# A convolution stage with one more shift copied by ScalarE, shifts loaded in two parts, and evictions in fixed places

## The chip, the core and the metric

The kernel runs on one core of a Trainium2 chip. A core has five engines that run side by side, each strictly in its own order: TensorE (PE in the profile, with its weight loads as PEld), VectorE (DVE), ScalarE (ACT), GpSimd (POOL) and SyncE (SP, which here only issues transfers). They wait for each other by semaphores. Sixteen DMA engines carry the transfers that SP and POOL issue. The metric is device time in microseconds for one execution; the time of a kernel is the median of its runs.

## What is computed

The input x has shape (4, 512, 512, 16): four images, 16 channels. Two layers are added to it.

```python
# layer 0: long convolution by FFT, all 16 channels mixed at each frequency
X = jnp.fft.rfft2(_gn(x), s=(1024, 1024), axes=(-3, -2))
Y = jnp.einsum('...hwi,ijhw->...hwj', X, H_full)      # H_full from a rational filter
x = x + jnp.fft.irfft2(Y, s=(1024, 1024), axes=(-3, -2))[..., :512, :512, :]
# layer 1: 3x3 convolution divided by the input's and kernel's norms, then arccos and tanh
x = x + _L1_conv_ref(_gn(x), kernel, bias, radius)
```

`_gn` is a group normalisation over eight groups of two channels. All arithmetic is in fp32.

## The kernel before

The kernel has four stages in time: the filter (up to some 3.6 ms), the forward transform of x along one axis, the convolution stage `conv_phase`, and the last stage with the second layer. The change lies in `conv_phase` alone.

`conv_phase` works through 513 rows (one row frequency each; the first is done as two). For a row, the other axis is split into two steps of a transform, 128 frequencies `f` by 8 taps, so that the long convolution becomes, at each `f`, a small product of input (`xe`) with filter (`gh`) over channels and taps. The parts of a row's work:

- `load_x`, `load_g`: the row of x and of the filter come from DRAM, through SP's queue.
- `turn_x` (ACT, then DVE): the row's own turning factors.
- `x_part`: four transforms of x on PE (tile `px`, two per buffer); each pair is evicted into `xe[:, 0]`, after b = 1 and after b = 3.
- `x_late` (POOL): `xe[:, 0]` is stored to DRAM (`xf_d`, first half); four multiplications into `xu`, one into `xl` and an addition make a turned copy `xl`, which is stored as the second half.
- Shifts: `xe` has eight slots t. Slot t needs slot 0 shifted by 16t partitions, with the partitions that fall off the end taken from `xl`. Slot 4 (64 partitions) is copied by ACT in two halves (`half_shift`, line 809: half 0 reads `xe`, half 1 reads `xl`). The other six are read back from `xf_d` by two loads of three slots each (`load_xe`, line 815), which need both stores.
- `g_part`: 32 matmuls on PE into `pg`, in four groups k, each evicted by two copies (c = 0 and 1) into `gh`.
- `mix`: 128 matmuls on PE, four groups of 32 (here M0 to M3) into `pm` (two buffers); each group is evicted into `yf`.
- `over_q`: 16 transposes in four groups into `pz`; for each group ACT copies one half to `zq` and DVE does five additions or subtractions (lines 874 to 878) into `z`. After the fourth group POOL computes `zd` and `z` (lines 882, 884).
- `over_g`: eight matmuls into `py`, one eviction to `yo`, and a store by POOL.

The evictions of `xe`, `gh`, `yf` and `yo`, 15 a row, go through `evict`, which gives every third to DVE and the others to ACT (lines 724 to 729):

```python
flip[0] += 1
if flip[0] % 3 == 0:
    nc.vector.tensor_copy(dst, src)
else:
    nc.scalar.copy(dst, src)
```

`step(n)` writes the parts of several rows in four quarters k: mixes of row n, `g_part` of row n + 1, `over_q` of row n - 1, `x_part` and `x_late` of row n + 2, `half_shift` of row n + 2 at k = 2 and 3, `over_g` of row n - 2. This program order is not the final one: when the program is built, the framework's scheduler puts each engine's instructions into an order of its own, and from then on that order is fixed. In the built program before, PE runs one mix group, then a `g_part` group, then a group of transposes, then px or py, and so on; ACT's copy of `xl` (half 1) stands ahead of evictions of `yf`, `gh` and `yo`. Buffers that matter: three of `xe`, two of `gh`, two of `pm`, three of `pg`, and three shared by `px`, `pz` and `py`.

Of the kernel before, what the change touches and what calls it, by code (L numbers as in the profile page):

```python
# [46 lines left out]
P = 128  # L47
N = 512
B = 4
C = 16  # L50
# [7 lines left out]
XF = F * 2 * B  # L58
XP = XF + 128
# [131 lines left out]
def load_const(nc, pool, cst, name, shape=None):  # L191
    src = cst[name]
    t = pool.tile(list(src.shape), F32, name=f"c_{name}")
    nc.sync.dma_start(out=t, in_=src)
    return t


def dram(t, row, offset, *dims):

    pitch = t.shape[1]  # L200
    lead = [[pitch, t.shape[0]]] if row is None else []
    return bass.AP(tensor=t.tensor, offset=t.offset + (row or 0) * pitch + offset,
                   ap=lead + [list(d) for d in dims])
# [492 lines left out]
def conv_phase(tc, cst, g_d, x_d, y_d):  # L696
    nc = tc.nc
    with ExitStack() as ctx:
# [15 lines left out]
        late = load_const(nc, cp, cst, "late").rearrange("p (v f) -> p v f", v=3)  # L714

        xf_d = [tc.dram_tile([16 * C, XP], F32, name=f"xf_d{n}") for n in range(4)]
# [2 lines left out]
        rows = [(0, 0, 0), (0, 0, 1)] + [(n // P, n % P, None) for n in range(1, N)]  # L719
        n_rows = len(rows)  # L720
        state = {}
        flip = [0]

        def evict(dst, src):
            flip[0] += 1
            if flip[0] % 3 == 0:
                nc.vector.tensor_copy(dst, src)  # L727
            else:
                nc.scalar.copy(dst, src)  # L729
# [13 lines left out]
        def load_x(n):  # L743
            rc, r, plane = rows[n]
            x = io.tile([P, B, 8 * C], F32, name="x")
            t, w = x.rearrange("p b x -> p (b x)"), B * 8 * C
            if plane is None:
                nc.sync.dma_start(out=t, in_=dram(x_d[rc], r, 0, [w, P], [1, w]))
            else:
                nc.gpsimd.memset(t[S:], 0.0)  # L750
                nc.sync.dma_start(out=t[:S], in_=dram(x_d[rc], r, plane * S * w, [w, S], [1, w]))
            state["x", n] = x
# [16 lines left out]
        def x_part(n, b):  # L769

            if b == 0:

                state["xe", n] = xep.tile([P, 8, F, 2, 2, 2], F32, name="xe")
            if b % 2 == 0:
                state["px"] = ps_f.tile([P, 2, F, 2], F32, name="px", tag="full")
            px = state["px"]
            nc.tensor.matmul(px[:, b % 2].rearrange("p f c -> p (f c)"), state["x", n][:, b],  # L777
                             state["dfs", n], start=True, stop=True)
            if b % 2:
                evict(state["xe", n][:, 0, :, b // 2], px.rearrange("p k f c -> p f c k"))  # L780
            if b == B - 1:
                del state["x", n], state["dfs", n]

# [22 lines left out]
        def half_shift(n, half):  # L806

            dst, src = ((slice(0, 64), state["xe", n][64:, 0]), (slice(64, P), state["xl"][:64]))[half]
            nc.scalar.copy(state["xe", n][dst, 4].rearrange("p f h c k -> p (f h c k)"),  # L809
                           src.rearrange("p f h c k -> p (f h c k)"))  # L810

        def load_xe(n):
            src = xf_d[n % 4]
            for t in (1, 5):
                nc.sync.dma_start(
                    out=state["xe", n][:, t : t + 3].rearrange("p t f h c k -> p t (f h c k)"),
                    in_=bass.AP(tensor=src.tensor, offset=src.offset + t * C * XP,
                                ap=[[XP, P], [C * XP, 3], [1, XF]]),
                )

        def g_part(n, j):


            if j % 4 == 0:
                state["pg"] = [ps_g.tile([P, 4, F], F32, name=f"pg{c}", tag="pg") for c in range(2)]
            g, pg = state["g", n], state["pg"]
            for c in range(2):
                half = slice(64 * c, 64 * c + 64)
                nc.tensor.matmul(pg[c][:, j % 4], g[half, j], dg[half], start=True, stop=True)  # L829
            if j == 3:  # L830
                state["gh", n] = ghp.tile([P, F, 2, C], F32, name="gh")
            if j % 4 == 3:
                for c in range(2):
                    evict(state["gh", n][:, :, c, j - 3 : j + 1], pg[c].rearrange("p j f -> p f j"))
            if j == C - 1:
                del state["g", n]

        def mix(n, g):

            if g % 8 == 0:  # L840
                state["pm"] = ps_m.tile([P, 8, 8, 2 * B], F32, name="pm")
            xe, gh, pm = state["xe", n], state["gh", n], state["pm"]
            for q in range(4):
                f = g + 32 * q
                nc.tensor.matmul(  # L845
                    pm[32 * q : 32 * q + 32, g % 8], gh[:, f].rearrange("p c j -> p (c j)"),
                    xe[:, :, f].rearrange("p t h c k -> p t (h c k)"), start=True, stop=True,
                )
            if g == 7:

                state["y", n] = yp.tile([P, 16, 32, 4], F32, name="yf")
            if g % 8 == 7:
                evict(state["y", n][:, :, g - 7 : g + 1].rearrange("p t g x -> p g t x"),
                      pm.rearrange("p g t (h x) -> p g (t h) x", h=2))
            if g == 31:
                del state["xe", n], state["gh", n]

# [30 lines left out]
        def over_g(n, k):  # L888

            rc, r, plane = rows[n]  # L890
            if k == 0:
                state["py"] = ps_f.tile([P, 2, 2, 8, C], F32, name="py", tag="full")
            z, d, py = state["z", n], state["zd", n], state["py"]
            odd, c2 = k // 2, k % 2
            for half in range(2):
                s0 = 2 * half + odd
                if s0 % 2 == 0:
                    zs = z[:, :, s0 + c2]
                elif s0 == 1:
                    zs = (d[:, :, 0], z[:, :, 5])[c2]  # L900
                else:
                    zs = (z[:, :, 4], d[:, :, 1])[c2]
                nc.tensor.matmul(  # L903
                    py[64 * half : 64 * half + 64, odd], ig[:, s0, c2],
                    zs.rearrange("p (t h) j -> p h t j", h=2),
                    start=(c2 == 0), stop=(c2 == 1),
                )
            if k < 3:
                return
            del state["z", n], state["zd", n]  # L910
            yo = yop.tile([P, 4 * P], F32, name="yo")
            evict(yo.rearrange("p (x j t) -> p x j t", x=4, j=C), py.rearrange("p o h t j -> p (o h) j t"))
            if plane is None:
                nc.gpsimd.dma_start(out=dram(y_d[rc], r, 0, [4 * P, P], [1, 4 * P]), in_=yo)
            else:
                for half in range(2):
                    nc.gpsimd.dma_start(
                        out=dram(y_d[rc], r, (64 * half + 32 * plane) * 4 * P, [4 * P, 32], [1, 4 * P]),
                        in_=yo[64 * half : 64 * half + 32],
                    )  # L920

        def step(n):


            def row(k):
                return 0 <= n + k < n_rows

            if row(3):
                load_x(n + 3)
            if row(2):  # L930
                load_g(n + 2)
            if row(1):
                load_xe(n + 1)
            for k in range(4):
                if row(0):
                    for g in range(8):
                        mix(n, 8 * k + g)
                if row(1):
                    for j in range(4):
                        g_part(n + 1, 4 * k + j)  # L940
                if row(-1):
                    for t in range(4):
                        over_q(n - 1, 4 * k + t)
                if row(2) and k == 0:
                    for m in range(2, B):
                        x_part(n + 2, m)
                    x_late(n + 2)
                if row(2) and k >= 2:
                    half_shift(n + 2, k - 2)
                if row(3) and k == 1:  # L950
                    turn_x(n + 3)
                if row(3) and k == 3:
                    for m in range(2):
                        x_part(n + 3, m)
                if row(-2) and k in (1, 2):
                    for m in range(2):
                        over_g(n - 2, 2 * (k - 1) + m)

        for n in range(-3, n_rows + 2):
            step(n)  # L960
# [479 lines left out]
```

## Time and profile before

| What | Value |
|---|---|
| median of three runs | 16334.61 us (16324.06 to 16345.95) |
| profiled execution | 16344.5 us, span 16342.7 us |
| busy, share of the span | PE 91%, DVE 64%, POOL 62%, ACT 54% |
| convolution stage | about 4630 to 13530 us |
| reads from DRAM, writes | 3030.71 MB, 1477.31 MB |
| loads of xe from xf_d | 1026 issues of 1536 KB |
| stores to xf_d | 1026 issues of 448 KB |
| one ACT eviction of 128x512 (gh) | 585 ns |
| one DVE eviction of 128x512 (gh) | 688 ns |
| one ACT copy of 64x1024 (slot 4) | 1.05 us |

The span is the time that the profile covers; the execution's own time lies 1.8 us above it. Busy shares are means over stages with different work, so the convolution stage has to be read by itself. In the lines of the time line the columns are start, duration, engine, source line, operation, tile written and read, shapes, and in brackets how long the engine stood idle before it and what released it. A released wait says who came last. "issue" stands for idle time in which nothing that the profile shows was waited for.

### The profile page before, as it was taken

To read this page: it belongs to the slowest core of one execution; us is meant where nothing else is said; L and a number is where in the kernel's file an instruction comes from. 1 tells how busy PE (TensorE), PEld (TensorE's weight loads), DVE (VectorE), ACT (ScalarE), POOL (GpSimd) and SP (SyncE) were. 2 spreads that over 40 slices of the span, in tenths; PEclk is the share of its full clock that TensorE was granted. 3 is DMA by queue.
4 is the path that set the end of the run, shared out by engine and by line. 5 is a ranking of instruction groups with operands and counts; after the bars stand their busy time and mean duration, and the time that the engine had idled before them with its cause. 6 is when DMAs were issued, how large, how long until landed. Compare 5 with 4: busy or idle time off the path is not lost. (4 is left out here: it accounts for less than half of the span.)

```text
span 16342.7 us, 538107 instructions
## 1 busy us (share of the span) xinstructions
PE 14869.0 (91%) x232588; PEld 10969.0 (67%) x232588; DVE 10396.8 (64%) x20763; ACT 8766.8 (54%) x17007; POOL 10169.4 (62%) x9645
## 2 busy tenths in 40 slices
PE   7999999999988888888888888888888888988888
PEld 5555555554566667766666676667666667877777
DVE  8999999984545555555555555555555552457887
ACT  4666666653345555555555555555555551027888
POOL 7777777763456666666666666666666660247766
PEclk8999999999999999999999999999999999989999
DMA  4888888888878888888888888888888886884531
GB/s 138 239 244 249 241 242 245 245 241 261 250 276 329 323 329 329 329 330 329 329 331 324 330 328 327 328 325 327 330 331 328 326 325 236 319 297 164 168 109 67
DMA packets 2914643, 4542.93 MB, mean 278 GB/s; under 512 B 126114, under 2 KB 2094460, under 8 KB 2801422
## 3 DMA queue, kind: packets, MB, share of 16 engines
q1 hardware_dynamic: 2703070, 3836.37, 67.9%
q0 software_dynamic: 172336, 605.00, 9.3%
q10 hardware_dynamic: 36864, 67.13, 1.2%
q8 instruction: 1831, 30.00, 0.7%
q14 instruction: 542, 4.44, 0.1%
HBM read 3030.71 MB, written 1477.31 MB: 276 GB/s over the span
## 5 line engine op out<-in xcount | busy, mean ns | idle before, releaser
L845 PEld LDWEIGHTS pm<-xe,gh 128*32 128x32 f32 x131328 | 2001.2, 111 | 1446.2 <-issue 1163.4
L845 PE MATMUL pm<-xe,gh 128*32 128x64 f32 x131328 | 2373.7, 222 | 650.1 <-issue 314.8
L829 PE MATMUL pg<-c_dg,g 64*128 64x128 f32 x32832 | 2599.4, 289 | 308.3 <-ACT gh L729 192.5
L874 DVE TENSOR_TENSOR z<-zq,pz 128x256 f32<-128x256 f32 x2052 | 861.6, 420 | 2952.0 <-ACT zq L873 2950.0
L829 PEld LDWEIGHTS pg<-c_dg,g 64*128 64x128 f32 x32832 | 2134.2, 190 | 573.3 <-ACT gh L729 245.9
L729 ACT COPY gh<-pg 128x512 f32<-128x512 f32 x2567 | 1446.9, 585 | 1296.4 <-PE pg L829 1293.9
L459 PE MATMUL pt<-ev_in,c_todd 128*128 128x512 f32 x4096 | 1924.7, 609 | 9.5 <-DMA ev_in<-g_d 9.5
L389 DVE RECIPROCAL dn<-dn 128x256 f32<-128x256 f32 x1024 | 1722.9, 1724 | 17.6
L390 POOL TENSOR_TENSOR sp<-m,dn 128x512 f32<-128x512 f32 x1024 | 1301.2, 1271 | 592.6 <-DVE dn L389 556.1
L809 ACT COPY xe<-xl 64x1024 f32<-64x1024 f32 x513 | 539.0, 1051 | 1883.2 <-POOL xl L800 1883.2
L727 DVE COPY gh<-pg 128x512 f32<-128x512 f32 x1537 | 1056.7, 688 | 663.5 <-PE pg L829 660.3
L866 PE MATMUL pz<-c_ident,yf 128*128 128x128 f32 x8208 | 1376.5, 291 | 19.4 <-issue 13.0
L798 POOL TENSOR_TENSOR xu<-xe,c_late 128x256 f32<-128x256 f32 x2052 | 1373.8, 692 | 20.5 <-DVE xe L727 6.4
L459 PEld LDWEIGHTS pt<-ev_in,c_todd 128*128 128x128 f32 x4096 | 728.9, 190 | 910.3 <-issue 773.0
L418 ACT COPY st<-pg 128x256 f32<-128x256 f32 x2048 | 616.8, 391 | 1301.6 <-PE pg L407 1301.6
L407 PEld LDWEIGHTS pg<-c_dinv,sp 64*128 64x128 f32 x16384 | 1005.6, 196 | 442.2 <-ACT sp L395 232.6
L800 POOL TENSOR_TENSOR xl<-xl,xu 128x1024 f32<-128x1024 f32 x513 | 1208.9, 2357 | 40.2
L407 PE MATMUL pg<-c_dinv,sp 64*128 64x128 f32 x16384 | 1108.3, 287 | 60.3 <-ACT sp L395 44.6
L882 POOL TENSOR_TENSOR zd<-z 128x512 f32<-128x512 f32 x513 | 654.1, 1275 | 781.6 <-DVE z L874 781.6
L903 PE MATMUL py<-z,c_ig 128*64 128x256 f32 x6156 | 1127.4, 397 | 6.6 <-issue 2.2
L1283 PE MATMUL pc<-l_band,xn 128*128 128x160 f32 (+2 forms) x6144 | 1075.8, 333 | 52.0 <-DVE e_o L1338 51.9
L777 PE MATMUL px<-dfs_n,x 128*128 128x256 f32 x4104 | 1080.4, 387 | 12.7 <-DMA c_late<-k_late 11.5
(211 smaller groups left out, 29585.0 us busy)
## 6 DMA issues: line engine op xcount, KB each, us to landing
xe<-xf_d SPq DMA_DIRECT2D x1026, 1536.0 KB
g<-g_d SPq DMA_DIRECT2D x511, 1024.0 KB
g_d<-st SPq DMA_DIRECT2D x256, 1024.0 KB
ev_in<-g_d SPq DMA_DIRECT2D x1024, 256.0 KB
g_d<-ot SPq DMA_DIRECT2D x1024, 256.0 KB
xf_d<-xe POOLq DMA_DIRECT2D x513, 448.0 KB, 8.3
xf_d<-xl POOLq DMA_DIRECT2D x513, 448.0 KB, 6.4
x_d<-xo SPq DMA_DIRECT2D x128, 1024.0 KB
```

Of the source, the lines that this page charges most:

```text
L389: nc.vector.reciprocal(dn, dn)
L390: nc.gpsimd.tensor_mul(w["sp"][:, v], w["m"][:, v], bc(dn, 2, [P, 2, 2, P]))
L407: nc.tensor.matmul(pg[u][:, n, k].rearrange("p a x -> p (a x)"), w["sp"][q, n, k, c, :], dinv[q, 2 * kp + k, c, :], start=(c == 0), stop=( ...
L459: nc.tensor.matmul(pt, todd[:, c, kc, hh * P : hh * P + P], ev[:, kc, c], start=(kc == 0), stop=(kc == 1),)
L729: nc.scalar.copy(dst, src)
L777: nc.tensor.matmul(px[:, b % 2].rearrange("p f c -> p (f c)"), state["x", n][:, b], state["dfs", n], start=True, stop=True)
L798: nc.gpsimd.tensor_mul(u[:, :, h, c], xe[:, :, h, 1 - c], bc(late[:, 1 + c], 2, [P, F, 2]))
L800: nc.gpsimd.tensor_add(xl.rearrange("p f h c k -> p (f h c k)"), xl.rearrange("p f h c k -> p (f h c k)"), u.rearrange("p f h c k -> p (f ...
L829: nc.tensor.matmul(pg[c][:, j % 4], g[half, j], dg[half], start=True, stop=True)
L845: nc.tensor.matmul(pm[32 * q : 32 * q + 32, g % 8], gh[:, f].rearrange("p c j -> p (c j)"), xe[:, :, f].rearrange("p t h c k -> p t (h c k ...
L866: nc.tensor.transpose(pz[:, t % 4].rearrange("p v q x -> p (v q x)"), y[:, at].rearrange("p g x -> p (g x)"), ident)
L903: nc.tensor.matmul(py[64 * half : 64 * half + 64, odd], ig[:, s0, c2], zs.rearrange("p (t h) j -> p h t j", h=2), start=(c2 == 0), stop=(c ...
```

## The change

- `evict` no longer counts; each call says whether DVE does it. On DVE: the eviction of px after b = 3, `gh` for c = 1, `yf` of M0 and M1, and `yo`: eight a row. On ACT: px after b = 1, `gh` for c = 0, `yf` of M2 and M3: seven a row. Before it was five and ten.
- Slot 2 (a shift by 32 partitions) is no longer loaded but copied by ACT in four pieces of 32 partitions (`quarter_shift`). Pieces 0 to 2 read `xe`, piece 3 reads `xl`. They are written at k = 0, 1 and 2 (two pieces). `half_shift` moves from k = 2 and 3 to k = 1 and 3.
- `load_xe` loads the five slots 1, 3, 5, 6 and 7, each in two parts cut where the partitions change from the first store to the second. The parts that need only the first store (`late` false) are issued at k = 3 of the step in which the row is stored, those that need the second at the start of the next step: ten issues a row for two.

Built, the orders differ from before by more than the edited lines. In the steady part PE runs M0 to M3 one after another; the groups of `g_part`, transposes, px and py stand between these blocks.

```diff
-        flip = [0]
-        def evict(dst, src):
-            flip[0] += 1
-            if flip[0] % 3 == 0:
+        def evict(dst, src, vector):
+            if vector:
                 nc.vector.tensor_copy(dst, src)
             else:
                 nc.scalar.copy(dst, src)
...
-                evict(state["xe", n][:, 0, :, b // 2], px.rearrange("p k f c -> p f c k"))
+                evict(state["xe", n][:, 0, :, b // 2], px.rearrange("p k f c -> p f c k"), b == 3)
...
-        def load_xe(n):
-            src = xf_d[n % 4]
-            for t in (1, 5):
+        def quarter_shift(n, q):
+            src = state["xl"][:32] if q == 3 else state["xe", n][32 * q + 32 : 32 * q + 64, 0]
+            nc.scalar.copy(state["xe", n][32 * q : 32 * q + 32, 2].rearrange("p f h c k -> p (f h c k)"),
+                           src.rearrange("p f h c k -> p (f h c k)"))
+
+        def load_xe(n, late):
+            for t in (1, 3, 5, 6, 7):
+                cut = P - t * C
+                p = slice(cut, P) if late else slice(0, cut)
                 nc.sync.dma_start(
-                    out=state["xe", n][:, t : t + 3].rearrange("p t f h c k -> p t (f h c k)"),
-                    in_=bass.AP(tensor=src.tensor, offset=src.offset + t * C * XP,
-                                ap=[[XP, P], [C * XP, 3], [1, XF]]),
+                    out=state["xe", n][p, t].rearrange("p f h c k -> p (f h c k)"),
+                    in_=xf_d[n % 4][t * C + p.start : t * C + p.stop, :XF],
                 )
...
-                    evict(state["gh", n][:, :, c, j - 3 : j + 1], pg[c].rearrange("p j f -> p f j"))
+                    evict(state["gh", n][:, :, c, j - 3 : j + 1], pg[c].rearrange("p j f -> p f j"), c == 1)
...
-                      pm.rearrange("p g t (h x) -> p g (t h) x", h=2))
+                      pm.rearrange("p g t (h x) -> p g (t h) x", h=2), g < 16)
...
-            evict(yo.rearrange("p (x j t) -> p x j t", x=4, j=C), py.rearrange("p o h t j -> p (o h) j t"))
+            evict(yo.rearrange("p (x j t) -> p x j t", x=4, j=C), py.rearrange("p o h t j -> p (o h) j t"), True)
...
-                load_xe(n + 1)
+                load_xe(n + 1, True)
...
-                if row(2) and k >= 2:
-                    half_shift(n + 2, k - 2)
+                if row(2) and k == 3:
+                    load_xe(n + 2, False)
+                if row(2):
+                    for q in ([0], [1], [2, 3], [])[k]:
+                        quarter_shift(n + 2, q)
+                    if k % 2:
+                        half_shift(n + 2, k // 2)
```

## The prediction

> **What bounds the kernel now.** I read four views in this order: busy time by stage, the waits inside the convolution stage, the time line of single rows there, and the durations of the copy that the change adds. The change touches one stage only, so the first question is how long that stage is and what its engines do. From the stage view (columns: stretch, length, busy us and count of PE, PEld, DVE, ACT, POOL, then granted clock, DMA share, GB/s):
>
> ```profile
> 8000.00:13000.00 5000.00, 4449.19 (x103874) 3485.20 (x103874) 2680.22 (x7503) 2627.07 (x4907) 3231.62 (x3175) 0.98 0.87 328
> ```
>
> No engine is full: PE 89%, POOL 65%, DVE 54%, ACT 53%, the DMA engines 87%. So what matters is who waits for whom. From the waits of 6000 to 12000 us (some 347 rows), and the entry of the partition copy, whose first and last start give the pace:
>
> ```profile
> ACT xe L809 <- POOL xl L800: 1277.8, 347, 6.5
> ...
> PE pm L845 <- issue: 201.1, 170, 2.6
> ...
> PE pm L845 <- DMA xe<-xf_d: 169.4, 108, 2.8
> ...
> PE pg L829 <- ACT gh L729: 131.4, 154, 3.7
> ```
>
> ```profile
> L809 ACT COPY xe<-xl x513: 1042/1050/1068, 4636.4 to 13504.4; 64x1024 f32<-64x1024 f32 x171
> ```
>
> 8868.0 us over 512 steps is 17.32 us a row. Every row ACT stands 3.7 us (1277.8/347) in front of the copy that reads xl, and everything queued behind it on ACT waits too. One such row, ACT and POOL:
>
> ```profile
> 7003.06 1.06 ACT L809 COPY xe<-xl 64x1024 f32<-64x1024 f32 x1 [3.71 <-POOL xl L800]
> 7004.15 0.58 ACT L729 COPY yf<-pm 128x512 f32<-128x512 f32 x1
> 7004.63 0.59 ACT L729 COPY gh<-pg 128x512 f32<-128x512 f32 x1
> 7005.10 0.39 ACT L873 COPY zq<-pz 128x256 f32<-128x256 f32 x1
> ...
> 7019.69 1.05 ACT L809 COPY xe<-xl 64x1024 f32<-64x1024 f32 x1 [3.74 <-POOL xl L800]
> ```
>
> ```profile
> 10006.03 1.28 POOL L882 TENSOR_TENSOR zd<-z 128x512 f32<-128x512 f32 x1
> 10007.40 1.29 POOL L884 TENSOR_TENSOR z<-z 128x512 f32<-128x512 f32 x1
> 10008.64 1.51 POOL L798 TENSOR_TENSOR xu<-xe,c_late 128x256 f32<-128x256 f32 x2
> 10010.10 0.56 POOL L791 DMA_DIRECT2D xf_d<-xe  x1
> 10010.68 1.35 POOL L798 TENSOR_TENSOR xu<-xe,c_late 128x256 f32<-128x256 f32 x2
> 10011.98 1.97 POOL L799 TENSOR_TENSOR xl<-xe,c_late 128x1024 f32<-128x1024 f32 x1
> 10014.03 2.36 POOL L800 TENSOR_TENSOR xl<-xl,xu 128x1024 f32<-128x1024 f32 x1
> ```
>
> This is a ring: xl ready, ACT copies it, then evicts the gh that PE needs, PE goes on to the transform of the next x (px), its eviction lets POOL store and multiply (6.29 us from 10010.10 to 16.39), xl ready again. It closes in 16.63 us (7003.06 to 7019.69). Rows in which a load of xe lands late take some 18.5 us instead; the mean is the 17.32. So a new order is judged by the length of its ring, not by busy time.
>
> **The change, part by part.**
>
> *Loads.* Six shifts of 0.5 MB become five, each in two parts: 3.1 MB a row becomes 2.6. The SP queue's share is 69.2% of the DMA engines for 4.45 MB a row (1544.03 MB over 347 rows), so the xe loads are about 8.5 us of the row's 15.1 busy us (0.87 × 17.32). By bytes they fall to 7.1; if each of the ten parts cost as much as a whole shift they would be 14.1, and the row's DMA 20.7 us. Ten issues for two on SP at 0.4 us (0.37 to 0.44 in the time line) are 3.2 us more on a queue that issues little else. I cost all this at nothing. Its cover: the built order puts the mixing that reads a part more than a row after its issue (the late parts are issued in the row after their store, and read at the end of the row after that). The 0.5 us a row (169.4/347) that PE waits for xe today goes.
>
> [...]
>
> *Copies.* ACT gets four 32x1024 copies. Nearest row: 64x1024 at 1.05 us. Ends: half of it if the time went with partitions, 1.05 if with the 1024 elements of each. I take 1.05, because 128x256 takes 0.39 and 128x512 0.58 on the same engine: length counts. That is 4.2 us, less three evictions at 0.585 handed to DVE: ACT goes from 9.1 us a row to 11.6, DVE from 9.3 by 3 × 0.687 to 11.4. Both fit into 17.3. What costs is where they stand.
>
> [...] By partitions alone the row sum below would be 0.5 us less.
>
> *Order.* The built program, whose engines run strictly in their own order, changes more than the diff says, the same in all but the first rows. PE now runs the four mixes of a row (M0 to M3, 32 matmuls each) one after another. pm has two buffers, so M2 waits until M0 is evicted, which is now always DVE's. In DVE's order that eviction stands behind: the first subtraction of the third group of over_q (waits for ACT's zq), the eviction of yo, and three more ops of that group. In ACT's order that zq stands behind: the copy of partitions 96 to 127 (q = 3, waits for POOL's xl), half_shift 1, and a gh eviction. And POOL's zd, at the head of its block, waits for the fourth group of over_q, whose transposes stand on PE behind M2, M3 and eight matmuls of g_part. So the new ring holds POOL's whole block. From xl ready, in us, with starts after each other as in the time lines above:
>
> - ACT: hand-over 0.03; q = 3 at 1.00 (pitch of two copies in a row; 1.05 long); half_shift 1.08 (7003.06 to 7004.15); gh pitch 0.47 (7004.63 to 7005.10); zq 0.39. Together 2.97.
> - DVE: 0.04 to start; first subtraction 0.34, yo 0.60, then 0.32, 0.32 and 0.20 for the three of the group; eviction of M0 0.69. Together 2.51, so 5.48. (Pitches from DVE's line there: 10007.85 to 08.19, 08.19 to 08.79, 10002.34 to 02.66 to 02.99 to 03.19.)
> - PE: 0.05; M2 and M3 1.03 each; seven matmuls of g_part 0.95; four transposes 0.66. Together 3.72, so 9.20.
> - ACT zq with hand-over 0.44, DVE subtraction 0.46, hand-over to POOL 0.10: 10.20.
> - POOL: 10.36 without a gap, 10006.03 to 10016.39, the block shown above. Its other inputs come in time: the eviction of px ends near 13.1, the store that needs it stands at 14.3.
>
> Ring: 20.56 us. In it PE has 14.9 us of work (four waves of 1.03 + 1.09, plus transposes, px and py), so it stands about 3.3 us before M2 and some more for gh evictions behind two of the new copies. PE's issue pauses in the mixes are 0.58 us a row (201.1/347); two of four mixes lie on the ring, and a PE that has just stood waiting should show fewer: I add 0.15, bounds 0 and 0.58. Six hand-overs could each be 0.1 off: ±0.5.
>
> Sum: 20.71 − 17.32 = 3.39 us over 512 rows, 1736 us. Stages before and after are not touched; the eight rows in which the order settles may give or take 30. The profiled execution took 16344.5 us (span 16342.7), 10 above the median: 18080, by the median 18070. Low end: q = 3 at half price and hand-overs 0.3 better, no pauses, 19.75 a row, 17580. High end: all pauses and hand-overs, 21.64, 18550.
>
> **Rivals.**
>
> 1. *Not slower* (the other side). M2 doesn't wait: the DVE eviction of M0 comes early, because xl is ready before ACT gets to it. Then PE goes from py straight through M0 to M3 and the row is PE's: 14.9 us of work, 1.6 us for the gh eviction behind the first two quarter copies, 0.7 for smaller waits: 17.2 us, 60 us less than now, 16270. For it: DMA waits vanish. Against it: POOL's block would have to begin over 3.3 us earlier, and it can't begin before the fourth group, that is, before M3. 5%.
> 2. *ACT's ring.* POOL is quicker than thought. The ring then runs from the subtraction of the fourth group (ends 10.10 in the list above) over the group's other four ops (11.2), the second px (starts 11.3, 1.03), its eviction on DVE (13.05) and, from 13.2 on ACT, three quarter copies, half_shift 0 and two gh evictions (4 × 1.0 + 2 × 0.5) to q = 3 at 18.2: 0.9 us a row more, 16800. Also slower, and the floor if only the xl wait falls. 6%.
> 3. *DMA takes over.* The parts cost more than whole shifts: at 14.1 us it only draws level with the ring (20.7), so it needs more still; at 16 us for the loads, 22.5 a row, 19000. 5%.
> 4. *The built order isn't what runs*: none; each engine's order is fixed.
>
> **How the numbers follow.** The forecast, with its bounds, gets 84%. A measurement can tell about 0.2% from no change here (the three times spread 0.13%). Slower: forecast, rivals 2 and 3, 95%; rival 1 is split, 4% faster and 1% the same. The range is the forecast's own, 17500 to 18550, which leaves out the rivals and the edges beyond the bounds, together under 20%.
>
> **What would show it.** Right: the pace of the copies of xl at 20.3 to 21 us; PE's largest wait before pm released by DVE's eviction of yf, some 3 us a row; POOL without gaps from zd to the add; ACT in front of the 32-partition copy from xl for about 2 us; waits of pm for DMA gone, DMA share near 0.65 to 0.7. Wrong: a row under 18 us with POOL idle inside its block, or waits of pm for DMA still there.

## The result: 20136.53 us, 23% slower

The changed kernel took 20136.53 us in the median of four runs (20062.22 to 20173.72), beside 16337.76 us for the kernel before (16324.06 to 16345.95, four runs): a ratio of 1.2321, 95% interval 1.2281 to 1.2360. The prediction was 18070 us with a range up to 18550. The sign was right, the size was not: 1735 us were forecast, 3799 came. The span of the profiled execution is 20171.7 us.

The stage view of the changed kernel, for the stretch that the prediction showed of before (length; busy us of PE, PEld, DVE, ACT, POOL; granted clock, DMA share, GB/s):

```profile
8000.00:13000.00 5000.00, 3685.95 (x72196) 2974.33 (x72192) 2804.71 (x5818) 2384.82 (x3612) 2237.17 (x2209) 0.88 0.80 207
```

PE fell from 89% to 74% busy, and its clock from 0.98 to 0.88. The DMA share fell only from 0.87 to 0.80, while the bytes per second fell by 37%: in a row the DMA engines move fewer bytes than before and yet are busy for 19.8 us (0.80 × 24.78) instead of 15.1. The entry of the copy that reads `xl` gives the pace:

```profile
L813 ACT COPY xe<-xl x513: 1042/1043/1057, 4634.1 to 17323.3; 32x1024 f32<-32x1024 f32 x171
```

12689.2 us over 512 steps is 24.78 us a row, against 17.32 before and 20.71 forecast. The waits from 7000 to 12000 us (us in total, times, longest), some 202 rows:

```profile
PE pm L849 <- issue: 519.4, 174, 6.5
ACT xe L813 <- POOL xl L798: 338.8, 201, 4.0
PE pg L833 <- ACT gh L727: 263.7, 201, 1.8
PE pm L849 <- DVE yf L725: 248.6, 180, 4.8
```

The first line is what the forecast missed: PE stands 2.57 us a row (519.4/202) inside the mixes and waits for nothing that the profile shows; before it was 0.58. No wait of `pm` for a load is left.

One whole turn of the ring in the time line of the changed kernel, cut to the steps that the prediction counted; ACT first, then DVE, PE and POOL:

```profile
10009.88 1.04 ACT L813 COPY xe<-xl 32x1024 f32<-32x1024 f32 x1 [1.73 <-POOL xl L798]
10010.93 1.04 ACT L807 COPY xe<-xl 64x1024 f32<-64x1024 f32 x1
10012.00 0.59 ACT L727 COPY gh<-pg 128x512 f32<-128x512 f32 x1
10012.49 0.38 ACT L877 COPY zq<-pz 128x256 f32<-128x256 f32 x1
...
10036.38 1.04 ACT L813 COPY xe<-xl 32x1024 f32<-32x1024 f32 x1 [1.44 <-POOL xl L798]
```

```profile
10012.90 0.42 DVE L878 TENSOR_TENSOR z<-zq,pz 128x256 f32<-128x256 f32 x1 [1.57 <-ACT zq L877]
10013.24 0.68 DVE L725 COPY yo<-py 128x512 f32<-128x512 f32 x1
...
10014.68 0.68 DVE L725 COPY yf<-pm 128x512 f32<-128x512 f32 x1
```

```profile
10012.51 2.00 PE L849 MATMUL pm<-xe,gh 128*32 128x64 f32 x128
10015.42 1.70 PE L849 MATMUL pm<-xe,gh 128*32 128x64 f32 x105 [0.91 <-DVE yf L725]
10021.27 0.86 PE L849 MATMUL pm<-xe,gh 128*32 128x64 f32 x23 [4.16 <-issue]
10022.07 2.07 PE L833 MATMUL pg<-c_dg,g 64*128 64x128 f32 x14
10024.07 1.11 PE L870 MATMUL pz<-c_ident,yf 128*128 128x128 f32 x4
```

```profile
10026.18 1.26 POOL L886 TENSOR_TENSOR zd<-z 128x512 f32<-128x512 f32 x1 [11.38 <-DVE z L878]
...
10033.91 2.43 POOL L798 TENSOR_TENSOR xl<-xl,xu 128x1024 f32<-128x1024 f32 x1
```

The records hold two entries for each matmul that the program writes (131328 at L849, for 513 rows of 128), so x128 are the 64 matmuls of two mix groups. From the start of the copy at 10009.88 to the end of M0's eviction at 10015.36 are 5.48 us, the forecast's figure to the hundredth. M2 starts 0.06 later, the fourth group of transposes ends at 10025.18: 9.76 us for a segment forecast at 3.67. From there to POOL's `zd` are 1.00 us, POOL's block takes 10.16 without a gap to the add's end at 10036.34, and ACT starts 0.04 later. The ring is the predicted one, segment by segment, and all the excess lies in PE's. Of that 6.1 us, 4.16 are the pause inside M3. The rest is PE itself being slow: the filter matmuls took 2.07 instead of 0.95, the transposes 1.11 instead of 0.66, M2 and M3 together 2.56 instead of 2.06.

The same five segments over all 201 turns between 7000 and 12000 us, worked out from the trace's starts and durations, are in the mean 5.56, 8.05 (PE's, with the hand-over of 0.06 to M2), 1.00, 10.23 and 0.03: 24.87 us. Of PE's 7.99 us from the start of M2 on, 5.00 are work and 2.99 are pauses of the kind "issue". So the pauses lie on the ring: of the 519 us of them inside the mixes, 517 stand behind the start of M2.

### The profile page after: what moved, and what is told of

It is laid out like the page before. It is cut to its first block, busy times and chain, and to the rows that moved or that the text cites. A ratio compares the mean times of both kernels' runs of the same rounds, so it can differ in the third digit from the quotient of the medians.

```text
span 20171.7 us, 549869 instructions
## 1 busy us (share of the span) xinstructions
PE 16324.1 (81%) x232588; PEld 12335.1 (61%) x232588; DVE 12779.1 (63%) x22302; ACT 10188.5 (51%) x17520; POOL 10141.6 (50%) x9645
## 5 line engine op out<-in xcount | busy, mean ns | idle before, releaser
L833 PE MATMUL pg<-c_dg,g 64*128 64x128 f32 x32832 | 3574.3, 320 | 1022.2 <-ACT gh L727 686.5
L833 PEld LDWEIGHTS pg<-c_dg,g 64*128 64x128 f32 x32832 | 3024.4, 219 | 1803.2 <-ACT gh L727 785.3
L849 PE MATMUL pm<-xe,gh 128*32 128x64 f32 x131328 | 2388.7, 232 | 1961.6 <-issue 1320.6
L725 DVE COPY gh<-pg 128x512 f32<-128x512 f32 x2052 | 1403.4, 684 | 3712.1 <-PE pg L833 3712.1
L849 PEld LDWEIGHTS pm<-xe,gh 128*32 128x32 f32 x131328 | 2137.8, 117 | 2145.1 <-issue 1366.5
L727 ACT COPY yf<-pm 128x512 f32<-128x512 f32 x1026 | 601.5, 586 | 3534.8 <-PE pm L849 3534.8
L764 DVE SCALAR_TENSOR_TENSOR dfs_n<-c_dfs,own,turn 128x256 f32<-128x256 f32 x513 | 1855.6, 3617 | 30.7 <-ACT turn L762 30.7
L813 ACT COPY xe<-xe 32x1024 f32<-32x1024 f32 x1539 | 1604.9, 1043 | 57.8 <-DVE xe L725 25.2
L775 PE MATMUL px<-dfs_n,x 128*128 128x256 f32 x4104 | 1246.3, 432 | 352.2 <-DVE z L882 318.6
L727 ACT COPY gh<-pg 128x512 f32<-128x512 f32 x2052 | 1199.3, 584 | 543.0 <-PE pg L833 517.2
L877 ACT COPY zq<-pz 128x256 f32<-128x256 f32 x2052 | 770.5, 375 | 1276.1 <-PE pz L870 1253.8
L907 PE MATMUL py<-z,c_ig 128*64 128x256 f32 x6156 | 1291.9, 455 | 6.2 <-DVE z L882 3.7
```

What stands on the lines that cost most here:

```text
L764: nc.vector.scalar_tensor_tensor(m, dfs[:, 0], own[:, 0, at], t, ALU.mult, ALU.add)
L813: nc.scalar.copy(state["xe", n][32 * q : 32 * q + 32, 2].rearrange("p f h c k -> p (f h c k)"), src.rearrange("p f h c k -> p (f h c k)"))
L849: nc.tensor.matmul(pm[32 * q : 32 * q + 32, g % 8], gh[:, f].rearrange("p c j -> p (c j)"), xe[:, :, f].rearrange("p t h c k -> p t (h c k ...
L907: nc.tensor.matmul(py[64 * half : 64 * half + 64, odd], ig[:, s0, c2], zs.rearrange("p (t h) j -> p h t j", h=2), start=(c2 == 0), stop=(c ...
```

## The experiments

Two questions: what makes PE pause ("loads": the two-part loads; "block": PE's order with the mixes in one block), and what slows PE where it doesn't pause. Row paces below are read as above, from the first and last copy of `xl`.

### Loads and order apart

`spread_whole` is the change with the five shifts loaded whole, after both stores:

```diff
-        def load_xe(n, late):
-            for t in (1, 3, 5, 6, 7):
-                cut = P - t * C
-                p = slice(cut, P) if late else slice(0, cut)
+        def load_xe(n):
+            src = xf_d[n % 4]
+            for t, m in ((1, 1), (3, 1), (5, 3)):
                 nc.sync.dma_start(
-                    out=state["xe", n][p, t].rearrange("p f h c k -> p (f h c k)"),
-                    in_=xf_d[n % 4][t * C + p.start : t * C + p.stop, :XF],
+                    out=state["xe", n][:, t : t + m].rearrange("p t f h c k -> p t (f h c k)"),
+                    in_=bass.AP(tensor=src.tensor, offset=src.offset + t * C * XP,
+                                ap=[[XP, P], [C * XP, m], [1, XF]]),
```

Built, its PE runs the mixes spread between the other groups, as before. `spread_parts` is the change itself, loads and all, with PE held to the order in which the program is written, which is also the spread one:

```diff
+        order = InOrder(tc, nc.tensor)
...
-            step(n)
+            with order:
+                step(n)
```

> The changed kernel with its five shifts loaded whole (slots 1, 3 and 5 to 7 in three loads after both stores). Built so, PE keeps one mix group at a time (M0, filters, transposes, px, M1, ...), as before the change. Evictions and the copies of slot 2 are as in the change. Theory 'block' (PE pauses because the four mix groups stand in one block): no pauses beyond the 0.58 us a row of before, row 16.5 to 18 us, 15900 to 16700 us. Theory 'loads' (PE pauses because the two-part loads hold up the DMA engines): the same here. Both fall if it takes over 19000 us: then the copies or the evictions are the cause.

> The changed kernel with PE held to the program's order, so that the mix groups stand apart again; two-part loads as in the change. Theory 'block': idle of PE before pm put down to issue falls from 2.6 us a row to under 0.8, row 17 to 18.5 us, 16200 to 16950 us. Theory 'loads': issue idle before pm stays above 2 us a row, and the DMA engines, busy 0.80 of 24.8 us a row in the changed kernel, set at least 19.8 us a row, 17600 us or more.

`spread_whole` took 16840.34 us (ratio 1.0291, 1.0274 to 1.0309), a row 18.28 us, a little above the range that both theories had named; `spread_parts` 18147.81 us (1.1095, 1.1079 to 1.1112), a row 20.80. The pauses and the SP queue (packets, MB, share of 16 engines) of both, 7000 to 12000 us; first `spread_whole`, some 273 rows:

```profile
PE pm L849 <- issue: 288.4, 328, 3.1
```

```profile
q1 hardware_dynamic: 267343, 1075.20, 59.4%
```

and `spread_parts`, some 240 rows:

```profile
PE pm L849 <- issue: 748.9, 336, 5.8
```

```profile
q1 hardware_dynamic: 261233, 942.60, 77.1%
```

In the steady rows of both, PE, ACT and DVE run the same groups in the same order. The two-part loads alone thus raise the pauses in the mixes from 1.06 to 3.12 us a row and cost 1307 us. Per row SP's queue takes 10.9 us of the DMA engines with whole loads (0.594 × 18.28) and 16.0 with parts (0.771 × 20.80), for the same bytes. Taken packet by packet from the trace, a 4 KB packet on that queue takes a median of 159 ns before and in `spread_whole`, 281 in `spread_parts` and 274 in the changed kernel. There are 640 such packets a row with five shifts and 768 with six, 128 for each shift, so they are the loads of `xe` alone. Other loads slow down beside them: the 2 KB packets of the load of x, which spans all partitions, take a median of 84 ns before and 159 in the changed kernel.

The order by itself, from the other side: `block_whole` has whole loads and the four mixes written in one block, in PE's program order; `block_parts` is the same with the change's two-part loads.

```diff
-                    for g in range(8):
-                        mix(n, 8 * k + g)
+            def mixes():
+                if row(0):
+                    for g in range(32):
+                        mix(n, g)
...
+            filters(2)
+            turns(2)
+            back(1)
+            mixes()
+            if row(2):
+                half_shift(n + 2, 1)
+            filters(3)
+            turns(3)
```

> Program rewritten so that PE's order has the four mix groups in one block, near the changed kernel's order, with whole loads. Theory 'block': issue idle before pm stays near 2.6 us a row, PE's clock falls behind it, row 24 to 25 us, 19800 to 20300 us. Theory 'loads': issue idle before pm under 0.8 us a row, row near the ring of 20.7 us, 17800 to 18400 us.

> The same rewritten program with the two-part loads: the control for the run with whole loads, and the nearest to the changed kernel. Both theories: near the changed kernel, 19600 to 20500 us, issue idle before pm 2 to 3 us a row.

`block_whole`: 19126.37 us (1.1697, 1.1680 to 1.1715), a row 22.74 us. `block_parts`: 19743.57 us (1.2072, 1.2054 to 1.2090), a row 23.94. The waits of `block_whole`, some 220 rows:

```profile
PE pm L849 <- DVE yf L725: 692.7, 219, 4.2
PE pm L849 <- issue: 8.2, 7, 2.3
```

Here is the forecast's own wait, 3.15 us a row (692.7/220) for M0's eviction, where it said "some 3 us"; and no pauses in the mixes, so blocks of mixes don't make PE pause. Still the row is 22.7 us and not 20.6, which "loads" had not expected. Its PE line says why:

```profile
10000.06 2.00 PE L849 MATMUL pm<-xe,gh 128*32 128x64 f32 x128
10005.83 3.64 PE L849 MATMUL pm<-xe,gh 128*32 128x64 f32 x128 [3.77 <-DVE yf L725]
10009.40 2.08 PE L833 MATMUL pg<-c_dg,g 64*128 64x128 f32 x16
10011.41 0.66 PE L870 MATMUL pz<-c_ident,yf 128*128 128x128 f32 x4
```

Matmuls of the same number and shape take 2.00 us ahead of the wait and 3.64 after it. This row is one of the slow ones: over all turns M2 and M3 take 2.94 us in the mean. The parts cost 617 us on top in this order and 1307 in the other. Over all of PE's lines they raise the pauses from 0.28 (60.8/220) to 1.36 us a row (285.0/209) here, and from 1.39 (378.4/273) to 3.98 (955.3/240) there; why by less in this order is open. `block_parts` stays 393 us below the changed kernel, with 1.04 us a row of pauses in the mixes (216.6/209), fewer than expected, against 2.57. Their PE orders differ in detail as well; what of that makes the difference is open.

### Does PE's clock account for the slow matmuls?

Repeated filter matmuls (each writes again what the original writes) keep PE at work while M2 waits. `block_warm` had 48 of them; `block_busy` 21 and `block_busy_short` 11, of one half of a filter group:

```diff
+            def one(c, times):
+                if row(1):
+                    half = slice(64 * c, 64 * c + 64)
+                    for _ in range(times if row(0) else 1):
+                        nc.tensor.matmul(state["pg"][c][:, 0], state["g", n + 1][half, 12], dg[half],
+                                         start=True, stop=True)
...
-            mixes()
+            mixes(range(16))
+            if row(1):
+                state["pg"] = [ps_g.tile([P, 4, F], F32, name=f"pg{c}", tag="pg") for c in range(2)]
+            one(0, 12)
+            mixes(range(16, 32))
```

> The run with the four mix groups in one block and whole loads (22.74 us a row), with 48 matmuls of g_part done again between M1 and M2, where PE stands 3.1 us a row for the eviction of M0. They write the same values once more and are on no other engine's way. Theory 'clock' (PE comes out of the wait at a lower granted clock and runs M2, M3 and g_part at about half speed, on the ring): M2 starts at the same place, M2 with M3 takes 2.1 us instead of 3.6, g_part 1.1 instead of 2.1, row 20.4 to 21.4 us, 17900 to 18450 us. Theory 'ring mis-sized elsewhere': the row stays at 22.5 or grows, 19000 us or more.

> The run with the mix groups in one block and whole loads, with 21 matmuls of g_part (one half, j = 12) done again between M1 and M2, 2.6 us by the 0.123 us that one took in the run before, into a buffer that DVE has long freed. M0 and M1 keep their place, and the repeats end before the wait for M0's eviction does. Theory 'clock': M2 with M3 takes 2.1 us instead of 3.6, the eight of g_part after it 1.1 instead of 2.1, row 20.4 to 21.6 us, 17900 to 18550 us. Theory 'ring mis-sized elsewhere': within 1% of the 19126 us without repeats.

> This is the change with whole loads and the four mixes in one block, and with eleven repeated filter matmuls (a repeat writes what its original wrote) between M1 and M2 instead of the 21 of the run before. In that run a repeat took 0.235 us, so that 21 of them (5.2 us) overran the wait of 3.16 us; eleven take 2.6 us and should end before M0's eviction. 'Clock' (the row of 22.7 us is longer than the predicted ring of 20.6 because PE runs at a lower clock after standing still for some 3 us): M2 and M3 2.0 us instead of 3.64, the eight filter matmuls after them 0.95 to 1.3 instead of 2.08, and with nothing overrun a row of 20.4 to 21.5 us, 17900 to 18500 us. 'Other' (something else makes the row longer than the ring): M2 and M3 quick, but the row stays above 22.2 us, over 18850 us. If M2 and M3 keep 3.6 us, the half of a wait without work is enough to slow PE and neither is told apart.

`block_warm` took 21824.61 us (1.3346, 1.3326 to 1.3366): its repeats filled 5.9 us, and its first filter group had moved ahead of M0, so that M0 waited for ACT. Its time settles nothing. `block_busy` took 19623.04 us (1.2016, 1.1998 to 1.2034): 5.17 us of repeats, so M2 started in the median 2.45 us after M0's eviction. `block_busy_short` took 18749.85 us (1.1458, 1.1438 to 1.1477), between what its two theories had named, with a row of 22.0 us. Its PE line:

```profile
10025.64 2.00 PE L849 MATMUL pm<-xe,gh 128*32 128x64 f32 x128
10027.57 2.94 PE L948 MATMUL pg<-c_dg,g 64*128 64x128 f32 x24
10031.35 2.00 PE L849 MATMUL pm<-xe,gh 128*32 128x64 f32 x128 [0.84 <-DVE yf L725]
...
10046.66 1.99 PE L849 MATMUL pm<-xe,gh 128*32 128x64 f32 x128
```

M2 and M3 take 2.00 us instead of 3.64 (in the mean over all turns 2.03 instead of 2.94), and M2 still waits here for the eviction, so the repeats add nothing to this row of 21.02 us (10025.64 to 10046.66). In the other turns they add little: in the median M2 starts 0.22 us after the eviction, against 0.06 without repeats. Over all turns PE's segment from M2 to the fourth transposes has a median of 3.67 us, exactly the forecast's sum, against 5.26 in `block_whole`; the stage's clock is 0.94 against 0.88, and the median row 21.2 us against 23.4. (Of the 0.6 us that are left over 20.56, ACT's and DVE's segment takes all: 6.10 instead of 5.48 in this written order.) The mean row is 22.0, because PE's pauses, now elsewhere than in the mixes, are 0.77 us a row (173.9/226 over all of PE's lines) against 0.28 (60.8/220); why the repeats bring more of them is open.

The granted clock in the trace says the same (columns as in the stage view, the clock third from the end). First `block_whole`: M0 with M1, then M2, M3 and the filter matmuls after them, then filter matmuls further on; and the whole row of `block_busy_short`:

```profile
10000.06:10002.06 2.00, 2.00 (x130) 1.83 (x128) 0.00 (x0) 1.96 (x3) 0.44 (x1) 1.00 0.52 152
10005.83:10011.30 5.47, 5.47 (x144) 5.18 (x144) 0.54 (x1) 1.17 (x2) 0.00 (x0) 0.50 0.98 341
10018.41:10020.41 2.00, 2.00 (x14) 1.78 (x14) 2.00 (x1) 1.96 (x3) 2.00 (x2) 0.50 0.59 192
```

```profile
10025.64:10046.66 21.02, 17.99 (x385) 14.94 (x383) 13.25 (x29) 11.95 (x19) 11.13 (x12) 1.00 0.67 246
```

M2 starts at half the clock in 108 of 219 turns of `block_whole` and in 2 of 225 of `block_busy_short`. So a PE that stands still for some 3 us and then works at half its clock is shown as the cause of `block_whole`'s slow matmuls.

In the changed kernel it is the pauses, not the wait for M0's eviction, that bring the half clock. M2 starts at half the clock in 1 of its 201 turns; in the turn shown above the clock is whole up to the pause inside M3 and half behind it:

```profile
10012.51:10017.10 4.59, 3.68 (x234) 3.43 (x234) 3.19 (x8) 1.28 (x4) 0.58 (x1) 1.00 0.74 212
10021.27:10025.18 3.91, 3.91 (x42) 3.51 (x42) 0.69 (x1) 1.17 (x2) 0.00 (x0) 0.50 0.13 20
```

The stretches at one clock, whole or half, all last whole multiples of 3.41 us between 7000 and 12000 us: 88 of them in the kernel before, 480 in the changed one. In `block_whole` the clock fell 2.48 us into the wait before M2 (10002.06 to 10004.54), and 1.71 us into the wait of 1.93 us in front of `gh` (10016.48 to 10018.19), behind which 14 filter matmuls took 2.07 us. At the same place of `block_busy_short`, after the same 1.93 us, the clock was whole and they took 1.16. These waits show no one length of standing after which the clock falls.

### What in the two-part loads makes packets slow

Ten loads of 64 partitions with `spread_whole`'s place and PE order, once of every second partition, once of neighbouring halves:

```diff
+            for t in (1, 3, 5, 6, 7):
+                for h in range(2):
+                    p = slice(h, P, 2)                  # spread_alternate
+                    p = slice(64 * h, 64 * h + 64)      # spread_halves
+                    nc.sync.dma_start(
+                        out=state["xe", n][p, t].rearrange("p f h c k -> p (f h c k)"),
+                        in_=xf_d[n % 4][t * C : t * C + P, :XF][p],
+                    )
```

> PE's mix groups apart, and each of the five shifts loaded after both stores by two loads of 64 partitions, the even ones and the odd ones: ten issues a row as in the change, the same bytes. Theory 'range' (a load of a short run of neighbouring partitions keeps the DMA engines longer for each packet, and so holds up PE's instructions): packets of 4 KB stay near the 159 ns of the run with whole loads, issue idle before pm under 1.5 us a row, row 18 to 19 us, 16700 to 17200 us. Theory 'number' (ten transfers a row cost more than three, however cut): packets of 4 KB over 230 ns or issue idle near 3 us a row, 17900 to 18300 us.

> The same with the halves of neighbouring partitions, 0 to 63 and 64 to 127. Theory 'range': packets of 4 KB over 220 ns, issue idle before pm 2 to 3.5 us a row, row 19.5 to 21 us, 17450 to 18250 us. Theory 'number': the same as the run with alternate partitions.

`spread_alternate`: 17103.89 us (1.0471, 1.0448 to 1.0493), a row 18.76 us. `spread_halves`: 17674.75 us (1.0814, 1.0796 to 1.0832), a row 19.85. The pauses and SP's queue, `spread_alternate` (some 267 rows) and then `spread_halves` (252):

```profile
PE pm L849 <- issue: 220.7, 281, 3.6
```

```profile
q1 hardware_dynamic: 289392, 1043.58, 56.7%
```

```profile
PE pm L849 <- issue: 594.8, 302, 4.4
```

```profile
q1 hardware_dynamic: 274289, 989.23, 72.8%
```

The same number of loads of the same size, with the same packets: 159 ns a packet over alternate partitions, 268 over neighbouring halves; pauses of 0.83 and 2.36 us a row. So it is the narrow run of neighbouring partitions of each load, not that there are ten. A load of neighbouring partitions also reads neighbouring rows of DRAM; which of the two sides makes its packets slow isn't told apart here. `spread_parts` takes 473 us more than `spread_halves`; its loads are of 16 to 112 partitions and half of them are issued earlier, and these two weren't separated either. Alternate halves are still 0.48 us a row slower than three whole loads, with fewer pauses; PE's waits for ACT's evictions of `gh` are 0.40 us a row longer (1.20, 320.9/267, against 0.80, 217.7/273), and why wasn't followed.

What links slow packets to PE's pauses is evidence from the records, not an experiment that isolates it. The trace has 16 KB packets on a queue of kind "instruction". Their median is 961 ns before, 948 in `spread_whole`, 1093 in `spread_parts` and 1185 in the changed kernel. After a pause in the mixes of `spread_parts`, PE goes on a nearly fixed time after such a packet has ended: 1461 ns in the median of 336 pauses, quartiles 1370 and 1569. From any moment back to the last such end it is 3702 ns, quartiles 1844 and 5938. The pauses of the runs without narrow loads end in the same way: after 1403 ns in the kernel before (141 pauses) and 1404 in `copies_alone` (260, see below). PE at a pause thus seems to be waiting for its own instructions; that these packets bring them is read from the queue's kind alone. The profile counts their time with that of the 16 DMA engines (q8: 568 packets and 0.9% of it in the changed kernel, 7000 to 12000 us). Slow packets can't be all that brings such pauses, since `copies_alone` has quick ones (medians of 159 ns for 4 KB and 947 ns for 16 KB).

### The rest of the change: copies and evictions

`evictions_alone` is the kernel before with the fixed evictions; `copies_alone` the kernel before with slot 2 copied and five whole shifts, in the places that the change has.

```diff
+                if row(2):
+                    for q in ([0], [1], [2, 3], [])[k]:
+                        quarter_shift(n + 2, q)
+                    if k % 2:
+                        half_shift(n + 2, k // 2)
```

> Before, with the evictions in fixed places alone. If the copies carry the 0.96 us a row by which the run with whole loads stays above before, this is within 1% of before (16200 to 16500 us). If the evictions carry it, 16650 to 16900 us.

> Before, with slot 2 copied by ACT and five whole shifts loaded, evictions by count as before. If the copies carry the 0.96 us a row, 16650 to 16950 us, with ACT's wait for xl ahead of two copies instead of one; if the evictions carry it, 16200 to 16500 us.

`evictions_alone`: 16395.13 us (1.0026, 1.0014 to 1.0038). `copies_alone`: 16721.74 us (1.0229, 1.0214 to 1.0245). Together they are most of `spread_whole`'s 2.9%, and the copies carry it; their pauses in the mixes are 1.48 us a row (409.4/277) against 0.6 before, though no load in them is narrow. Why is open.

### Taking the wait for xl away

The copies of `xl` stand at the end of POOL's block, on ACT. Three kernels (the kernel before, `copies_alone`, `spread_whole`) got them one step later, at k = 0, with PE and ACT held to the program's order. By a slip of placement they stood after the next `x_late` and so read the `xl` of the following row, which isn't what the reference computes.

> Before, with half_shift 1 (the copy that reads xl) moved one step later, PE and ACT held to the program's order. If the ring through ACT's wait for xl sets before's clean rows (16.63 us): that wait disappears, row 15.5 to 16.9 us, 15400 to 16150 us, and the load of xe is the next to be late. If something else sets them: within 1% of before, or slower by what the pinned order costs.

> The same idea with slot 2 copied by ACT and five whole shifts loaded; the two copies that read xl stand one step later. DMA work falls from 15.1 to about 14.3 us a row, ACT is busy 11.9 us a row. If waits on loads limit the run without the copies, this is faster than it, 15300 to 16000 us; if ACT's added 2.8 us do, slower, 16000 to 16700 us.

> The last one with the evictions in the change's fixed places, so all of the change but the two-part loads, with the readers of xl one step later. If ACT's load limits, faster than the one without fixed evictions by up to 0.5 us a row (three evictions leave ACT): 15200 to 16300 us.

They took 17178.66 us (1.0505, 1.0489 to 1.0520), 18763.05 (1.1478, 1.1461 to 1.1495) and 17981.16 (1.0999, 1.0981 to 1.1017). ACT waited for `xl` in every row (7.8 us a row in the first, 2050.9/264), so the wait had been made longer, not removed; they say only that.

With the copies ahead of `x_late` they read their own row's `xl`; PE and ACT are held to program order:

```diff
+                if row(1) and k == 0:
+                    quarter_shift(n + 1, 3)
+                    half_shift(n + 1, 1)
...
                 if row(2):
-                    for q in ([0], [1], [2, 3], [])[k]:
+                    for q in ([], [0], [1, 2], [])[k]:
                         quarter_shift(n + 2, q)
-                    if k % 2:
-                        half_shift(n + 2, k // 2)
+                    if k == 3:
+                        half_shift(n + 2, 0)
```

> Before, with the copy that reads xl one step later and ahead of the next xl, so that it reads the row's own xl; PE and ACT in the program's order. If the ring through ACT's wait for xl sets before's clean rows (16.63 us), the wait for xl on ACT is gone and the row takes 15.5 to 17 us, 15400 to 16200 us; the load of xe is then what is late. If not, within 1% of before or slower.

> The same with slot 2 copied by ACT (its piece from xl also one step later) and five whole shifts. If loads of xe limit the run without these copies, faster than it by up to 0.7 us a row (DMA work 14.3 instead of 15.1 us); if ACT does, slower.

> The same with the change's fixed evictions too: everything of the change but the two-part loads, with the readers of xl one step later. 15300 to 16400 us; faster than the one with counted evictions if ACT limits that.

`read_next_step` (the kernel before, only `half_shift` 1 moved): 16396.48 us (1.0041, 1.0026 to 1.0056). `read_next_step_copies` (slot 2 copied, five whole shifts): 16215.5 us (0.9924, 0.9907 to 0.9940). `read_next_step_fixed` (the fixed evictions as well: the whole change but its two-part loads): 16200.12 us (0.9919, 0.9904 to 0.9934), a row 17.02 us. PE's largest wait before `pm` in the first and in the last of them (some 287 and 294 rows):

```profile
PE pm L845 <- DMA xe<-xf_d: 278.4, 123, 4.9
```

```profile
PE pm L849 <- issue: 336.7, 265, 3.7
```

ACT's wait for `xl`, 3.7 us a row before, is gone from all three, and moving it alone, with the two engines' order held, gains nothing, though 15400 to 16200 us had been expected: the loads of `xe` then land last (0.97 us a row, 278.4/287). With five whole shifts and the copies that wait goes too, and the row is quicker than before by 0.3 us, though PE now pauses 1.15 us a row in the mixes (336.7/294). The fixed evictions add nothing clear: the intervals of the last two overlap. `read_next_step_fixed` is the best version found, 0.8% below the kernel before.

## Why the prediction was right in kind and wrong in size

*Right.* The 32-partition copy: 1.04 us, "I take 1.05". The ring's path, and of its five segments four within 0.2 us. "POOL without gaps", the wait of ACT in front of the 32-partition copy (1.68 us a row, 338.8/202, for "about 2"), and the waits of `pm` for DMA gone. Rivals 1 and 2 are excluded by the row of 24.8 us.

*Wrong, and the largest: "a PE that has just stood waiting should show fewer: I add 0.15, bounds 0 and 0.58".* Inside the mixes the pauses measured 2.57 us a row, over all of PE's lines 3.02 (610.5/202), and nearly all of them (2.99 a turn) lie on the ring: just behind the wait that was to make them fewer. The row that the argument leaned on, 0.58 us in the kernel before, was itself a measure of loads that span all partitions, and the change replaces just these.

*Wrong, beneath that: "I cost all this at nothing"*, for the loads. The cover named was real: between 7000 and 12000 us no reader waited for a part. But the cover was against late landing only. In the changed kernel SP's queue takes 16.1 us a row (0.651 × 24.78), and the 4 KB packets, which are the loads of `xe`, 11.7 us of it: nearer the upper bound of 14.1 than the 7.1 by bytes. Whole loads take 7.4 us in `spread_whole`, counted in the same way, and the six shifts before the change 8.3, beside the 8.5 of the prediction. The DMA share was therefore 0.80 and not "near 0.65 to 0.7". Rival 3 carried the right suspicion with the wrong mechanism: over the stage the DMA engines were not full (0.80), and no wait for a load set the row. In `spread_alternate`, whose ten loads each reach across the partitions, the 4 KB packets take 159 ns in the median, as with whole loads.

*Wrong, the smaller: the segment "M2 and M3 1.03 each; seven matmuls of g_part 0.95; four transposes 0.66", priced at the durations of a PE that hardly stands still.* PE's 7.99 us from M2 on hold 5.00 us of work, 1.33 more than the 3.67 forecast. Of the 5.00 us, 2.44 ran at half the clock, and 2.05 of these in stretches that begin within a pause. By `block_whole`'s 3.64 to 2.00 us that accounts for some 1.10 of the 1.33; the rest isn't traced. So in this kernel the slow work follows from the pauses. The forecast put no price on it, although it put a wait of 3.3 us in front of M2: where that wait came true, in `block_whole`, the same segment took 5.26 us in the median.

In the changed kernel M2's wait is 1.23 us a row (248.6/202) for "some 3". The filter matmuls and `py` ahead of M0 are slow as well (2.08 us for the 16 from 10035.04, where `block_busy_short` has 1.66; the clock is half from 10034.09 to 10037.50), so M0 ends later and less of the wait is left.

The sum for the rows from 7000 to 12000 us: 20.56 forecast without pauses, 2.99 of pauses and 1.33 of slow PE are 24.88, measured 24.87; the other segments are within 0.13 of the forecast. Over 512 rows that is some 1660 us for the longer ring that was forecast (512 × 3.24), 1530 for the pauses and 680 for slow PE; less some 45, since the mean row of the whole stage is 0.09 us shorter than those of this window, some 3825, as the two spans differ (20171.7 − 16342.7 = 3829).

## What to carry to other kernels

Cutting a load at a partition boundary to start part of it early can cost far more than the lateness it removes (here 617 and 1307 us in the two orders, where PE's waits for `xe` had been 0.5 us a row): look at what its packets take, and at PE's own pauses, not only at who waits for the data. If a change puts a regular wait of some microseconds in front of TensorE, or pauses of that length inside its work, price the matmuls behind them at the slow rate seen here (M2 and M3 3.64 us for 2.00), and look whether other matmuls can stand in the wait (with eleven repeats there, 2.03 us in the mean for 2.94). A copy that reads the last product of another engine's long block is better read one step later than waited for, but its gain only shows when the next wait is removed in the same edit (here a ratio of 1.0041 alone, 0.9924 with a shift less to load).

## What else the runs showed

An operation on DVE stretched eightfold in the changed kernel. Its entry before and after (least, median and greatest ns):

```profile
L766 DVE SCALAR_TENSOR_TENSOR dfs_n<-c_dfs,own,turn x513: 477/479/2548, 4618.9 to 13463.1; 128x256 f32<-128x256 f32 x171
```

```profile
L764 DVE SCALAR_TENSOR_TENSOR dfs_n<-c_dfs,own,turn x513: 474/3742/3778, 4616.6 to 17267.9; 128x256 f32<-128x256 f32 x171
```

In the new order it falls beside POOL's operations for `xl` (10003.89 to 10007.63 in the row above, POOL's from 10002.27 on). In 503 of 513 rows it took over 3 us, each time with such work beside it, some 3.5 us of it in the mean; where no work of POOL ran beside it, in 507 rows before and 9 after, it took at most 485 ns. The operation stands off the ring here, and the ring's segment on ACT and DVE is near its forecast (5.56 us for 5.48); on the ring it would have cost an estimated 3.3 us (3742 less 479 ns).
